# Two graph layers with neighbour lists: 114 list rounds in place of 119

## The chip, the cores and the metric

The kernel runs on one core of a Trainium2 chip. The metric is the device time of one execution in microseconds (us). The engines are TensorE (PE; its weight loads appear as PEld), VectorE (DVE), ScalarE (ACT), GpSimd (POOL) and SyncE (SP), which issues most of the DMAs.

## The reference

There are 3,327 nodes with 512 features each, and one adjacency matrix `adj` of 3,327 x 3,327. It is sparse and very uneven: the chance of an entry falls with the product of the roots of row and column number, so the first nodes have many neighbours and the last ones few. Cut to what matters:

```
h = relu(layernorm(x))
x = x + adj @ (relu(adj @ (h @ W1) + b1) @ W2) + b2            # layer 0
h = relu(layernorm(x))                                          # layer 1
ts     = adj @ h
attn_k = sigmoid([ts, h] @ W_k.T + b_k)                         # k = a, b: one number a node
s      = s_left[i] + s_right[j]                                 # from h @ W_sa and a_sa
e      = where(adj != 0, exp(-leaky_relu(s)), 0)
x_a    = (e / sum(e)) @ (h @ W_sa)
x_b    = adj @ (h @ W_gcnb) + b_gcnb
x = x + sigmoid(attn_a * x_a + attn_b * x_b)
```

Layer 1 needs, for every node, two weighted sums over its neighbours' rows of `h`: one with `adj`, one with `e`.

## The kernel before

The nodes are padded to 3,328 and cut into 26 blocks of 128. `adj` comes in transposed, and its columns (the nodes that receive) are cut into seven chunks: six of 512 and one of 256.

**First pass** (L494 to L536). For every chunk `c` the loop over the 26 blocks `j` loads a tile of `adj` (L510), multiplies it into `acc_u` (L511), and finds for each group of 32 columns the largest entry of each row (`most`, L515). From `most` the generator `make_lists` (L384) builds, one chunk later and a step at a time (`next(lists)`, L520), the list of the rows that have any entry in a group of 32 columns. These lists are what the change is about.

- A list has a fixed room: `rooms[i]` (L42) is the number of **rounds** of block `i`, and each round holds 64 entries (HALF) of each of the block's four groups of 32 columns. The four groups lie as two halves of the partitions (h) and two columns (q). Block 0, the hub, has no lists (0 rounds) and is computed densely. Places that a list doesn't fill get a row number beyond the matrix.
- In `make_lists` lists are built in batches of up to 18 rounds (`CW // NT`, L432), a batch being several (block, q) pairs. For each pair VectorE makes two threshold tiles `at` (L447), TensorE multiplies them into `p_list` (L459, two matmuls for each round and q), and for each batch VectorE runs five operations: `past` (L465), its sum `jb` (L470), and L471, L475 and L478, which leave row numbers in `row_h` and `row_a`. Between these steps the generator yields.
- `size` compares every list's length with its room (L414), and `overflow` is their maximum (L685).

GpSimd gathers by these row numbers (`gather`, L138; every gather in the profile has line L139). `gather_adj` (L148) yields, for blocks 1 to 25 in this order, one gather for each round and q: 128 pieces of 32 numbers of `adj` into the block's buffer `ae[i]`; pieces beyond the matrix are skipped, and the buffer was cleared before (L381). `gather_behind` (L173) issues one such gather at a time, tied behind a matmul of the dense passes: after two of three matmuls in the first pass (L521), after four of five in the second (L670).

**Second pass** (L658 to L699). The same tiles of `adj` are loaded again and multiplied into `acc_g` (L665). When a chunk is done, `make_h1` (L572) finishes layer 0 for its blocks, makes layer 1's `h`, and writes each block's rows, with one score as 513th column, to `h_rows` in DRAM (L588). In between, `add_hubs` (L619) sums up the hub block.

**Last stage** (L747 to L967). Blocks are taken from 25 down to 1. For each block:

- `attend` (L756) goes by segments of up to four rounds (`segments`, L121). For each round two gathers fetch 128 rows of 520 numbers each from `h_rows` (L774), places that are not filled fetching the last row (L475). Each round goes to one of 16 pairs of row buffers, which are used in turn (`pairs`, L753), so a gather waits until the sums of 16 rounds before have read its buffer. A block's first gather is also tied to the sums of three or four blocks before (`LEAD`, L777 to L779). Then VectorE and ScalarE compute `e` for the segment (L780, L784, L206 to L208, L789).
- `sums` (L796) adds up both sums in two PSUM banks: for each round four matmuls of 64x64 by 512 (L811), one for each quadrant of the array. In float32 each is two instructions in the profile, so a round is eight.
- `copy_out` (L880), `turn` (L816, transposes `ptt`, L823), `weigh` (L854: products `p_b`, L863, and `p_a`, L870) and `finish` (L719) make the output of a block. The loop at L918 writes the order out by hand: the products of the block before last stand ahead of the transposes of the last and of this block's sums. Block 1 (L941 to L967) has its segments' sums split: the first ahead of block 2's products, the others after.

If `overflow` is set, a branch at L970 computes layer 1 once more, densely, for all blocks. For the inputs given here the lists, counted with the reference's inputs, all fit into their rooms, before and after the change.

Of the kernel before, what the change touches and what calls it, by code (L numbers as in the profile page):

```python
# [37 lines left out]
def list_rooms(n_blocks):  # L38

    rooms = [0, 10, 8, 7, 6, 6] + 5 * [5] + 12 * [4]  # L42
    return (rooms + n_blocks * [3])[:n_blocks]


# [1 line left out]
def kernel(  # L47
# [23 lines left out]
    NCH = len(chunks)  # L71
    NG = NP // GW
    rooms = list_rooms(NB)
    first = [2 * sum(rooms[:i]) for i in range(NB)]
    NL = 2 * sum(rooms)
# [1021 lines left out]
```

## Time and profile before

| | |
|---|---|
| three runs | 788.9, 789.4 and 790.33 us, median 789.4 us |
| span of the profiled execution | 861.4 us |
| mean granted TensorE clock | 0.973 of full speed |
| TensorE busy | 796.8 us (92%) |
| VectorE, ScalarE, GpSimd busy | 519.0 (60%), 187.8 (22%), 514.0 us (60%) |
| DMA | 202.82 MB, 235 GB/s on average |
| first pass; second pass; last stage | until about 234; until about 448; until 861 us |
| gathers of `adj` (`ae`, L139) | 238, from 76.4 to 446.0 us |
| gathers of `h` rows (`hr` and `rows`, L139) | 150 and 88, from 459.9 to 817.5 us |
| sums at L809 | 952 instructions, 137.8 us busy in all |

The table is read from the page's first three parts and from the timeline. In the groups of instructions each row gives line, engine, operation, output and inputs with partitions x elements, count, busy time in us, mean ns of one, and the idle time ahead with what ended it. L809 is the matmul statement that begins there. Matmuls overlap, so the sum of the single durations is more than the busy time. A profiled execution is longer than a plain one.

### The profile page before, as it was taken

How to read it: one execution, taken by the hardware profiler on the slowest of the kernel's cores; microseconds unless marked ns; L12 is line 12 of the kernel's file. 1: busy time of each engine (PE TensorE's matmuls, PEld its weight loads, DVE VectorE, ACT ScalarE, POOL GpSimd, SP SyncE). 2: the span in 40 equal slices, each digit the busy share in tenths (PEclk: the TensorE clock that was granted, in tenths of full speed). 3: DMA queues.
4: the chain of work that ended last, by engine and by line, in shares of the span. 5: the costliest groups of instructions: out<-in, count | busy, mean ns of one | idle time of the engine just before them, and what ended most of it. 6: DMA issues, size and time to landing. Idle time of an engine off the chain costs nothing.

```text
span 861.4 us, 12424 instructions
## 1 busy us (share of the span) xinstructions
PE 796.8 (92%) x3707; PEld 426.9 (50%) x3707; DVE 519.0 (60%) x1668; ACT 187.8 (22%) x396; POOL 514.0 (60%) x533
## 2 busy tenths in 40 slices
PE   9999899999798999999989599699999999999795
PEld 8774444444443444444454366356555555445454
DVE  6777899998645776586565455254453534345342
ACT  6770000000002233033042022112221212112112
POOL 2302666666677777677755666676666767667600
PEclk9999999999799999999999799899999999999899
DMA  7787998887588998999957667777777777767620
GB/s 240 242 272 220 314 316 245 279 281 233 159 278 261 337 326 287 313 329 301 324 163 239 174 202 208 243 202 222 222 212 230 202 220 207 226 194 206 186 71 29
DMA packets 108220, 202.82 MB, mean 235 GB/s; under 512 B 17490, under 2 KB 31345, under 8 KB 108145
## 3 DMA queue, kind: packets, MB, share of 16 engines
q1 hardware_dynamic: 72800, 124.40, 44.0%
q0 software_dynamic: 26656, 66.41, 27.9%
q10 hardware_dynamic: 8688, 11.15, 3.9%
q8 instruction: 31, 0.51, 0.2%
q14 instruction: 45, 0.36, 0.1%
HBM read 182.22 MB, written 20.55 MB: 235 GB/s over the span
## 4 chain that ended last, share of the span: by engine, by line
PE 76%; DVE 8%; issue 6%; DMA 6%; ACT 1%; another core or an unknown queue 1%; SPq 0%; POOL 0%; DVEq 0%; POOLq 0%; ACTq 0%
PE acc L809 15%; PE acc_u L511 13%; PE p_b L863 12%; PE p_a L870 11%; PE acc_g L665 10%; DMA a<-in_adjT_dram 4%; PE acc_hub L624 3%; PE ptt L823 3%; DVE most L515 3%; PE pu L293 3%; PE p_list L459 2%; PE px L580 2%; DMA xb<-in_x_dram 1%; PE pt L285 1%; PE awake L100 1%
## 5 line engine op out<-in xcount | busy, mean ns | idle before, releaser
L139 POOL DMA_INDIRECT ae<-in_adjT_dram,row_a x238 | 256.2, 1076 | 161.6 <-issue 62.4
L139 POOL DMA_INDIRECT hr<-h_rows,row_h x150 | 154.6, 1031 | 70.5 <-issue 35.7
L511 PE MATMUL acc_u<-a,rows 128*128 128x512 f32 (+1 forms) x364 | 166.5, 588 | 3.2 <-DMA a<-in_adjT_dram 3.2
L665 PE MATMUL acc_g<-a,g 128*128 128x512 f32 (+1 forms) x364 | 157.9, 572 | 6.8 <-DMA a<-in_adjT_dram 6.6
L863 PE MATMUL p_b<-W_g_sb,tyT 128*128 128x257 f32 x416 | 105.6, 398 | 21.2 <-issue 20.2
L139 POOL DMA_INDIRECT rows<-h_rows,row_h x88 | 90.8, 1032 | 55.7 <-issue 18.9
L515 DVE TENSOR_REDUCE most<-a 128x16 f32<-128x512 f32 (+1 forms) x182 | 111.1, 639 | 7.7 <-DMA a<-in_adjT_dram 4.5
L665 PEld LDWEIGHTS acc_g<-a,g 128*128 128x128 f32 x364 | 67.7, 192 | 85.3 <-issue 62.6
L863 PEld LDWEIGHTS p_b<-W_g_sb,tyT 128*128 128x128 f32 x416 | 78.3, 194 | 57.6 <-issue 29.9
L870 PE MATMUL p_a<-W_sa_sb,tyT 128*128 128x512 f32 (+2 forms) x216 | 94.8, 582 | 1.0 <-issue 1.0
L511 PEld LDWEIGHTS acc_u<-a,rows 128*128 128x128 f32 x364 | 65.4, 196 | 50.5 <-issue 42.7
L809 PE MATMUL acc<-hr,ae 64*64 64x512 f32 x600 | 84.4, 608 | 2.6 <-issue 2.2
L838 DVE COPY tyT<-ptt 128x512 f32<-128x512 f32 x51 | 34.8, 685 | 68.4 <-PE ptt L823 27.6
L870 PEld LDWEIGHTS p_a<-W_sa_sb,tyT 128*128 128x128 f32 x216 | 41.4, 192 | 40.4 <-issue 38.5
L809 PE MATMUL acc<-rows,ae 64*64 64x512 f32 x352 | 53.4, 596 | 2.9 <-issue 2.8
L809 PEld LDWEIGHTS acc<-hr,ae 64*64 64x64 f32 x600 | 34.8, 136 | 36.5 <-issue 33.8
L208 DVE SCALAR_TENSOR_TENSOR ae<-ae 128x256 f32<-128x256 f32 (+2 forms) x36 | 12.8, 377 | 61.8 <-ACT ae L207 39.2
L728 ACT ACTIVATE f<-f 128x2 f32<-128x2 f32 x26 | 5.3, 203 | 192.1 <-DVE vb L734 71.6
L302 ACT ACTIVATE gT<-acc_u,b_col 128x512 f32<-128x512 f32 (+1 forms) x7 | 4.6, 657 | 163.9 <-issue 78.7
L735 DVE TENSOR_TENSOR vb<-p_b,bg_row 128x257 f32<-128x257 f32 x26 | 11.1, 426 | 42.9 <-PE acc L809 28.6
L559 DVE SCALAR_TENSOR_TENSOR junk<-rows,w_rows 128x512 bf16<-128x512 f32 x52 | 35.6, 685 | 1.7 <-ACT rows L201 0.3
L583 DVE TENSOR_TENSOR xb<-px,xb 128x512 f32<-128x512 f32 x26 | 17.0, 684 | 31.3 <-PE px L580 22.7
(142 smaller groups left out, 936.4 us busy)
## 6 DMA issues: line engine op xcount, KB each, us to landing
a<-in_adjT_dram SPq DMA_DIRECT2D x325, 256.0 KB
h_rows<-rows SPq DMA_DIRECT2D x26, 260.0 KB
x<-in_x_dram SPq DMA_DIRECT2D x26, 256.0 KB
xb<-in_x_dram SPq DMA_DIRECT2D x26, 256.0 KB
x<-xb ACTq DMA_DIRECT2D x26, 256.0 KB
x1b<-x SPq DMA_DIRECT2D x26, 256.0 KB
out_dram<-va SPq DMA_DIRECT2D x25, 256.0 KB
ae<-in_adjT_dram,row_a POOLq DMA_INDIRECT x238
```

Source lines behind the costliest of these rows:

```text
L139: return nc.gpsimd.indirect_dma_start(out=dst, out_offset=None, in_=table, in_offset=bass.IndirectOffsetOnAxis(ap=rows, axis=0), bounds_ch ...
L293: nc.tensor.matmul(pu[:, :HID], hT[:, k, :], W1_sb[:, k, :], start=(k == 0), stop=(k == KD - 1))
L511: added = nc.tensor.matmul(acc[:, :w], u[j], a[:, :w], start=(j == 0), stop=(j == NB - 1))
L515: nc.vector.tensor_reduce(most[:, : w // GW, j], a[:, :w].rearrange("p (b i) -> p b i", i=GW), axis=AX.X, op=ALU.max, apply_absolute_value ...
L559: return nc.vector.scalar_tensor_tensor(junk, h, 1.0, w_rows[:, s, :], op0=ALU.mult, op1=ALU.mult, accum_out=into)
L624: nc.tensor.matmul(acc_hub[k], s, hrow[i % NR][:, :D], start=(i == 0), stop=(i == NB - 1))
L665: added = nc.tensor.matmul(acc[:, :w], g[j], a[:, j % per, :], start=(j == 0), stop=(j == NB - 1))
L809: added = nc.tensor.matmul(taken[i]["acc"][h][q * HALF : (q + 1) * HALF, :], both[half_p, q * n + k, :], taken[i][k0][k][half_p, q, :D], s ...
L823: moved = nc.tensor.transpose(pt[:, k * P : (k + 1) * P], ty[h][:, k * P : (k + 1) * P], ident)
L838: last = nc.vector.tensor_copy(dst, src)
L863: nc.tensor.matmul(p_b[n][:, :WH], tyT[:, k, 0, :], W_g_sb[:, k, n * WH : (n + 1) * WH], start=(k == 0), stop=(k == KD - 1),)
L870: last = nc.tensor.matmul(p_a[:, c0:c1], tyT[:, k, 1, :], W_sa_sb[:, k, c0:c1], start=(k == 0), stop=(k == KD - 1),)
```

## The change

One line of `list_rooms` is changed:

```diff
-    rooms = [0, 10, 8, 7, 6, 6] + 5 * [5] + 12 * [4]
+    rooms = [0, 9, 8, 7, 6, 6] + 5 * [5] + 8 * [4]
     return (rooms + n_blocks * [3])[:n_blocks]
```

Block 1 has nine rounds in place of ten, blocks 19 to 22 have three in place of four, and all other blocks what they had: 119 rounds become 114. The rooms set, besides the sizes of several buffers,

- the number of gathers: two of `adj` and two of `h` rows for each round, so 228 and 228 in place of 238 and 238;
- the number of matmuls: four list matmuls and four sums (eight instructions) for each round;
- the segments: block 1's are three, three and three rounds in place of four, three and three; blocks 19 to 22 keep one each;
- the batches in which lists are built: chunk 0 (blocks 1 to 3) has batches of 18, 16 and 14 rounds in place of 10, 18, 15 and 7; chunk 4 has 16 and 14 in place of 16 and 16; chunk 5 has 18 and 6 in place of 16 and 14;
- which of the 16 row buffers a block's rounds get, since fewer are taken before it.

SyncE's instructions are the same in number, kind and order, and so are ScalarE's, but for five smaller shapes.

## The prediction

> **What bounds the kernel now.** I read the profile in this order: the page's chain that ended last, the groups of instructions, the chain in order of time for the last stage, GpSimd's timeline there, and busy time by windows.
>
> ```profile
> PE 76%; DVE 8%; issue 6%; DMA 6%; ACT 1%; another core or an unknown queue 1%; SPq 0%; POOL 0%; DVEq 0%; POOLq 0%; ACTq 0%
> ...
> L809 PE MATMUL acc<-hr,ae 64*64 64x512 f32 x600 | 84.4, 608 | 2.6 <-issue 2.2
> ...
> L809 PE MATMUL acc<-rows,ae 64*64 64x512 f32 x352 | 53.4, 596 | 2.9 <-issue 2.8
> ```
>
> TensorE carries three quarters of the path. The 119 rounds are its 952 matmul instructions of L809: eight each, 137.8 us together, 1.16 us a round on average. The chain in order of time shows what one round is worth (start, length, what):
>
> ```profile
> 507.50 2.63 PE acc L809 x22
> 510.13 3.67 PE p_b L863 x16
> 513.80 3.43 PE p_a L870 x8
> 518.32 3.49 PE acc L809 x30
> 521.81 1.28 PE p_b L863 x5
> 523.28 2.63 PE p_b L863 x11
> 525.92 3.43 PE p_a L870 x8
> 530.43 3.49 PE acc L809 x30
> ```
>
> Block 23 (three rounds) starts its sums at 507.50 and block 22 (four) at 518.32; the next start is 530.43. TensorE goes from sums to products to sums with hardly a gap, so this stage is bound by TensorE. Three rounds take 2.63 us, four 3.49: 0.87 us a round. The end of the kernel reads the same way, with block 1's first segment of four rounds at 827.95 and its other six at 838.75:
>
> ```profile
> 827.95 3.49 PE acc L809 x30
> 831.44 3.67 PE p_b L863 x16
> 835.10 3.43 PE p_a L870 x8
> 838.75 5.31 PE acc L809 x46
> ```
>
> GpSimd, which issues the gathers, is not the bound of the four-round blocks:
>
> ```profile
> 519.58 1.00 POOL L139 DMA_INDIRECT hr<-h_rows,row_h  x1 [0.30 <-issue]
> 520.88 0.99 POOL L139 DMA_INDIRECT hr<-h_rows,row_h  x1 [0.30 <-issue]
> 523.83 0.99 POOL L139 DMA_INDIRECT hr<-h_rows,row_h  x1 [1.96 <-remote]
> 525.13 1.00 POOL L139 DMA_INDIRECT hr<-h_rows,row_h  x1 [0.31 <-issue]
> ```
>
> A gather goes out every 1.30 us, eight in 10.4 us, and then GpSimd waits 1.4 to 2.7 us once in each block, for sums that free a row buffer or that its pace is tied to. The last view is one window of 5 us (busy time of PE, PEld, DVE, ACT and POOL, clock, DMA share, GB/s):
>
> ```profile
> 480.00:485.00 5.00, 0.00 (x0) 0.00 (x0) 0.00 (x0) 0.00 (x0) 3.00 (x3) 0.50 0.72 200
> ```
>
> Here TensorE, VectorE and ScalarE all stand still while gathers go on. Two more such stops lie near 549 to 559 and 797 to 808.
>
> **What the Trainium skill says.** "TensorEngine Tiling (Array Packing)", Tiling Modes: the array can work as four independent 64x64 tiles. The trace agrees: 32 instructions of some 589 ns each take 3.49 us, 109 ns apart. "DMA: Bandwidth & Descriptors", SWDGE vs HWDGE vs iDMA: descriptors of DMAs issued from GpSimd are made by software on that engine; the trace's 1.0 us for every gather, empty or full, agrees. "Runtime: NRT & Kernel Launch", Instruction fetch mechanics: each engine's instructions are fetched by DMA in blocks of 16 KiB. The page of before has an instruction queue with 31 packets for 0.51 MB, 16.5 KB each. I take this as a possible cause of the stops; no run shows it.
>
> **The change, part by part.**
>
> Lengths, counted from the inputs: block 1's longest list has 529 entries, room falls from 640 to 576; the longest in blocks 19 to 22 has 183, room falls from 256 to 192. So no list overflows, the branch at L970 is not taken, and all ten removed gather pairs were padding: the adjacency rows lie out of bounds, the feature rows all point at row 3327.
>
> 1. Blocks 19 to 22, one round less each. Starts of sums of three-round blocks lie 10.91 and 10.82 us apart (496.59, 507.50, 518.32). Those of eight four-round blocks away from the stops lie 12.11, 11.93, 11.97, 11.99, 12.24, 11.86, 11.94 and 12.33 apart, 12.05 on average. The difference is 1.18 us: 0.87 of sums, and 0.31 of gaps inside the products (as at 521.81 to 523.28) that three-round blocks do not show. I take 1.18; bounds 0.87 (the gaps stay) and 1.18. Four blocks: 4.7 us.
> 2. Block 1, nine rounds. Its segments go from 4, 3, 3 to 3, 3, 3, so the first sums lose a round, 0.87 us; VectorE is done with them before 829, and with the later segments by 834.7, 4 us before they are used. The upper bound is 1.18. 0.9 us.
> 3. The gathers. Ten feature gathers of 128 rows of 2,080 bytes go, 13 us of GpSimd's cadence and 2.7 MB. Hidden: GpSimd waits for TensorE in each of these blocks. Ten adjacency gathers go from the two dense passes, where each is paced behind a matmul (L525, L671); the last now goes out at 446.0, at the end of the pass, and will go out about 12 matmul steps earlier. The next work on that queue is the first feature gather at 459.9, which waits for the last h_rows, so this gains nothing.
> 4. The lists. In chunk 0 four batches (10, 18, 15, 7 rounds) become three (18, 16, 14). By the rows of L465, L470, L471, L475 and L478 for these shapes VectorE's work falls from 5.9 to 5.0 us; chunks 4 and 5 save 0.1 and 0.3 (16 and 14 become 16 and 14; 18 and 6). The threshold operations L447 stay (380 ns at 640, 296 at 256, 304 at 192). TensorE loses 20 list matmuls, 0.5 us at about 25 ns apart. Together 1.8 us in the first pass, where VectorE is 93% busy (97.5 of 105 us from 102 to 207) and the chain changes between it, TensorE and loads. The first lists are now made a step later, but the first gather's slot in the loop (j = 4) is the same. Bounds: 0 and 1.8; I take 0.5.
> 5. VectorE and ScalarE also lose about 0.7 and 0.06 us per shortened block. Hidden: VectorE is busy 6.4 of 12.1 us in that window. Clearing smaller buffers on GpSimd lies before its first gather at 76.4, for which it waited 47 us: nothing.
>
> The sum is 4.7 + 0.9 + 0.5 = 6.1 us from the profiled span of 861.4 us. The three plain runs are 72 us shorter (789.4), and what makes up that difference is not known from here; the saved work is array time at full clock, so I take the same 6.1 us from 789.4: **783.3 us**. With all bounds low it is 4.4 us (785.0), with all high 4 x 1.18 + 1.18 + 1.8 = 7.7 us (781.7).
>
> **Rivals.**
>
> - *The gathers bind without the profiler.* For: between waits they go out without a pause, and the DMA engines are 71 to 79% busy here. Against: GpSimd waits in every block, and blocks of three rounds, 7.8 us of gathers, take 10.9. Then 10 x 1.30 = 13 us go: 776.4.
> - *The head start is lost again.* In blocks 10 to 6 (five rounds) ten gathers take 13.0 us and a wait of some 1.8 follows, in a period of about 14.6, with TensorE at half pace in the first sums. If TensorE arrives there earlier and only waits longer for rows, points 2 and 4 stay: 1.4 us, 788.0. Against: GpSimd has eight gathers less to make before, 10.4 us.
> - *One stop more (the slower side).* Each stop costs about 10.4 us on TensorE (476.4 to 486.8). If they depend on where instruction refills meet dense gathers, about 100 fewer TensorE instructions shift where they fall. One more anywhere after 460 gives 789.4 - 6.1 + 10.4 = 793.7. It decides once added stop time exceeds 6.1 us. For: three in 390 us; against: nothing shows that their number follows the instruction count, or that they occur without the profiler.
> - *One stop fewer*: 789.4 - 6.1 - 10.4 = 772.9.
> - *The branch is taken after all*: 7 x 26 x 8 dense matmuls at 0.86 us, 1,250 us more. The counted lists exclude it.
>
> **How the numbers follow.** Chances: the sum 0.66; gathers bind 0.08; head start lost 0.09; a stop more 0.10; a stop fewer 0.07. I leave out the last two, 0.17: the range is 776.4 to 788.0, and the likeliest case's own is 781.7 to 785.0. A change of over 0.2%, 1.6 us, is about what a measurement of this kernel can tell from none. Faster: 0.66 + 0.08 + 0.07 = 0.81; within 0.2%: 0.09; slower: 0.10.
>
> **What would show it.** Right: sums of blocks 22 to 19 with 24 instructions in about 2.63 us and starts about 10.9 us apart; block 1's first sums 2.6 us; chunk 0's lists in three batches; 912 instructions at L809. Wrong: starts still 12 us apart in those blocks (a wait took the place), longer gaps ahead of sums at five-round blocks (head start lost), a fourth stop of all three engines, or a drop near 13 us. Point 4 is wrong if the first pass ends later than 234 us.

## The result, and the profile after

The changed kernel takes 781.3 us (median of four runs, 779.5 to 783.3) against 789.9 us; the ratio is 0.988, 95% interval 0.983 to 0.993. A second measurement gave 0.988 again (0.985 to 0.991), 9.7 us. The forecast was 783.3 us, 6.1 us faster.

The profiled execution of after has a span of 780.7 us and lies within the plain runs, so a profiled execution isn't longer as such. That of before, 861.4 us, was an unusually slow one: a second profile of the same kernel (before_again, below) has 797.6 us, and the three stops are not in it. So before is read from before_again from here on. First the chain that ended last and the groups of sums, of after:

```profile
span 780.7 us, 12235 instructions
...
PE 82%; DMA 7%; DVE 7%; issue 1%; ACT 1%; POOL 0%; SPq 0%; POOLq 0%; ACTq 0%; DVEq 0%
...
L809 PE MATMUL acc<-hr,ae 64*64 64x512 f32 x560 | 68.0, 607 | 0.0
...
L809 PE MATMUL acc<-rows,ae 64*64 64x512 f32 x352 | 42.5, 594 | 2.5 <-issue 1.8
```

There are 912 instructions at L809, 110.5 us busy, 0.97 us a round in place of the 1.16 of the first profile. The same lines of before_again give 116.3 us for 119 rounds, 0.98 us: most of the fall from 137.8 us is the disturbance, not the change. The chain in order of time of after (start, length, what), at blocks 23 and 22:

```profile
478.06 2.63 PE acc L809 x22
480.69 3.67 PE p_b L863 x16
484.35 3.43 PE p_a L870 x8
488.87 2.63 PE acc L809 x22
491.50 3.67 PE p_b L863 x16
495.17 3.43 PE p_a L870 x8
```

Block 22 now has 22 pieces in 2.63 us, and starts are 10.81 us apart. In before_again four-round blocks start 11.67 us apart, without the gap inside the products, as here at block 22:

```profile
498.09 3.49 PE acc L809 x30
501.58 3.67 PE p_b L863 x16
505.25 3.43 PE p_a L870 x8
509.76 3.49 PE acc L809 x30
```

The difference is 0.86 us, TensorE's work alone.

GpSimd's timeline shows what the first profile hid. This is before_again, at blocks of four rounds and near the end:

```profile
540.06 1.00 POOL L139 DMA_INDIRECT rows<-h_rows,row_h  x1 [0.30 <-issue]
541.37 1.00 POOL L139 DMA_INDIRECT rows<-h_rows,row_h  x1 [0.30 <-issue]
542.68 1.00 POOL L139 DMA_INDIRECT hr<-h_rows,row_h  x1 [0.30 <-issue]
543.98 1.00 POOL L139 DMA_INDIRECT hr<-h_rows,row_h  x1 [0.30 <-issue]
...
717.35 1.00 POOL L139 DMA_INDIRECT hr<-h_rows,row_h  x1 [0.30 <-DMA hr<-h_rows,row_h]
718.65 1.00 POOL L139 DMA_INDIRECT hr<-h_rows,row_h  x1 [0.30 <-PE acc L809]
```

From 451.14 to 765.74 no gather after the first starts more than 0.31 us after the one before has ended; most go out 1.30 us apart, the farthest 1.82. GpSimd never waits for sums: **it is behind**, and the 238 gathers take 314.6 us. After has pauses again, in its three-round blocks:

```profile
498.37 0.99 POOL L139 DMA_INDIRECT hr<-h_rows,row_h  x1 [0.30 <-issue]
502.68 0.99 POOL L139 DMA_INDIRECT hr<-h_rows,row_h  x1 [3.31 <-PE acc L809]
```

Here a gather waits 3.31 us for sums of an earlier block: the stream has caught up. After 502.68 no gather waits any more. Now the end of the stage in the chain in order of time. Before_again, blocks 4 to 2:

```profile
714.16 4.43 PE acc L809 x38
718.59 0.06 issue
718.65 5.01 DMA hr<-h_rows,row_h
...
730.47 1.25 issue
731.72 3.77 DMA hr<-h_rows,row_h
...
736.99 4.06 DMA hr<-h_rows,row_h
...
744.59 1.76 issue
746.35 9.67 PE acc L809 x64
```

And after_again (a second profile of after):

```profile
706.45 5.21 PE acc L809 x46
711.66 3.67 PE p_b L863 x16
...
719.84 6.06 PE acc L809 x54
725.90 3.67 PE p_b L863 x16
...
734.11 1.27 issue
735.38 7.10 PE acc L809 x64
```

A "DMA hr" piece is a gather's flight, from its issue at 718.65 to its landing at 723.66, on which a block's scores wait. In before_again the chain leaves TensorE at block 4 and runs through gathers until block 2's sums. It puts the gather of 718.65 down to sums that ended at 718.59, but that gather goes out 1.30 us after the last, as any other: the sums didn't hold it up. In after_again the chain stays on TensorE, but for 1.27 us ahead of block 2's sums. There, too, their scores have just waited for a gather:

```profile
733.33 0.23 DVE L780 TENSOR_TENSOR ae<-s_left,hr 128x64 f32<-128x64 f32 x1 [2.33 <-DMA hr<-h_rows,row_h]
```

How much of this TensorE itself stands still is in busy time by windows, of before_again and then of after_again, over blocks 4 to 2 (columns as in the prediction):

```profile
715.00:747.00 32.00, 27.71 (x174) 16.29 (x170) 14.21 (x54) 6.26 (x14) 24.69 (x25) 0.96 0.81 219
```

```profile
706.00:736.00 30.00, 28.70 (x191) 17.19 (x193) 15.37 (x56) 6.26 (x14) 22.99 (x24) 1.00 0.81 223
```

TensorE idles 4.3 us of the first and 1.3 us of the second. But the wait costs more than that. Block 2's sums, 64 instructions, take 9.67 us in before_again and 7.10 in after_again. This is the start of them in before_again:

```profile
746.35:751.00 4.65, 4.65 (x24) 1.68 (x28) 3.81 (x13) 0.20 (x1) 3.72 (x4) 0.50 0.94 296
```

TensorE is busy throughout, but at a granted clock of 0.50 (the third number from the end). In gathers_only (below), where TensorE doesn't stop ahead of these sums, the clock there is 1.00 and they take 6.92 us. So in this execution the late gathers cost 4.3 us of standing still and about 2.75 us of slow sums, 7 us in all. After's first profile lies between: 1.77 us of waiting ahead of block 2, then 8.79 us of sums.

From the first gather of h rows to the end, before_again takes 346.5 us, after 338.8 and after_again 339.8.

### The profile page after: what moved, and what is told of

Read it like the earlier page. It is cut to its first block, busy times and chain, and to the rows that moved or that the text cites. A ratio compares the mean times of both kernels' runs of the same rounds, so it can differ in the third digit from the quotient of the medians.

```text
span 780.7 us, 12235 instructions
## 1 busy us (share of the span) xinstructions
PE 755.4 (97%) x3647; PEld 415.5 (53%) x3647; DVE 517.5 (66%) x1658; ACT 185.5 (24%) x396; POOL 489.8 (63%) x513
## 4 chain that ended last, share of the span: by engine, by line
PE 82%; DMA 7%; DVE 7%; issue 1%; ACT 1%; POOL 0%; SPq 0%; POOLq 0%; ACTq 0%; DVEq 0%
PE acc_u L511 16%; PE acc_g L665 14%; PE acc L809 13%; PE p_b L863 12%; PE p_a L870 11%; DMA a<-in_adjT_dram 6%; PE ptt L823 3%; PE pu L293 3%; PE acc_hub L624 2%; PE px L580 2%; PE p_list L459 2%; PE pt L285 1%; DVE junk L559 1%; DVE xb L583 1%; PE awake L100 1%
## 5 line engine op out<-in xcount | busy, mean ns | idle before, releaser
L139 POOL DMA_INDIRECT ae<-in_adjT_dram,row_a x228 | 244.2, 1071 | 145.2 <-DVE most L515 49.1
L139 POOL DMA_INDIRECT hr<-h_rows,row_h x140 | 143.5, 1025 | 47.0 <-issue 27.4
L511 PE MATMUL acc_u<-a,rows 128*128 128x512 f32 (+1 forms) x364 | 164.0, 580 | 1.5 <-DMA a<-in_adjT_dram 1.5
L863 PE MATMUL p_b<-W_g_sb,tyT 128*128 128x257 f32 x416 | 97.1, 386 | 0.8 <-ACT tyT L836 0.5
L863 PEld LDWEIGHTS p_b<-W_g_sb,tyT 128*128 128x128 f32 x416 | 76.6, 189 | 30.8 <-DVE ae L206 7.3
L809 PE MATMUL acc<-hr,ae 64*64 64x512 f32 x560 | 68.0, 607 | 0.0
L809 PE MATMUL acc<-rows,ae 64*64 64x512 f32 x352 | 42.5, 594 | 2.5 <-issue 1.8
L809 PEld LDWEIGHTS acc<-hr,ae 64*64 64x64 f32 x560 | 29.8, 136 | 23.4 <-issue 22.9
L302 ACT ACTIVATE gT<-acc_u,b_col 128x512 f32<-128x512 f32 (+1 forms) x7 | 4.6, 656 | 154.8 <-PE acc_u L511 97.9
L696 DVE TENSOR_TENSOR xb<-xb,b_row 128x512 f32<-128x512 f32 x26 | 17.7, 690 | 29.7 <-DMA xb<-in_x_dram 24.1
L823 PEld LDWEIGHTS ptt<-ident,ty 128*128 128x128 f32 x208 | 24.2, 141 | 14.2 <-issue 12.9
```

Source lines behind the costliest of these rows:

```text
L139: return nc.gpsimd.indirect_dma_start(out=dst, out_offset=None, in_=table, in_offset=bass.IndirectOffsetOnAxis(ap=rows, axis=0), bounds_ch ...
L511: added = nc.tensor.matmul(acc[:, :w], u[j], a[:, :w], start=(j == 0), stop=(j == NB - 1))
L809: added = nc.tensor.matmul(taken[i]["acc"][h][q * HALF : (q + 1) * HALF, :], both[half_p, q * n + k, :], taken[i][k0][k][half_p, q, :D], s ...
L823: moved = nc.tensor.transpose(pt[:, k * P : (k + 1) * P], ty[h][:, k * P : (k + 1) * P], ident)
L863: nc.tensor.matmul(p_b[n][:, :WH], tyT[:, k, 0, :], W_g_sb[:, k, n * WH : (n + 1) * WH], start=(k == 0), stop=(k == KD - 1),)
```

## The experiments

Each ratio is to the kernel before; times in us are the ratio applied to its median in the same measurement (793.8 to 794.1 us). Single profiles of one kernel differ by several us in where the last stage begins, so totals are taken from the timed runs and the profiles are read within a stage.

### before_again and after_again: the two kernels once more

> The kernel before, unchanged: a second profile and the spread of the measurement. If the three stops of TensorE, VectorE and ScalarE in the profile of before belong to that one execution, this profile has a span near 788 us, four-round blocks 11.7 us apart in place of 12.05, and a ratio of 1.000 within 0.2%. If they belong to the kernel, the span is again near 860 us.

Measured: 1.000 (0.998 to 1.002), span 797.6 us. The stops belong to the one execution; the four-round period is 11.67 us, as expected for that case.

> The changed kernel again, for a narrower interval. Sum of the parts (work of five rounds on TensorE 4.3 us, lists 0.5 to 1.8 us): 4.8 to 6.1 us below before, ratio 0.992 to 0.994. If gathers bind (13 us) 0.983; if the 8.5 us measured first are real, 0.989.

Measured: 0.988 (0.985 to 0.991), 9.7 us. The interval, 7.1 to 12.3 us, leaves out both the sum of the parts and ten gathers' 13 us.

### late_only and early_only: the two halves of the change

late_only keeps lists of 119 rounds and issues the ten empty gathers of adj into a spare buffer; `used` holds the shorter rooms:

```diff
-        n = -(-rooms[i] // SEG)
-        cuts = [-(-rooms[i] * k // n) for k in range(n + 1)]
+        n = -(-used[i] // SEG)
+        cuts = [-(-used[i] * k // n) for k in range(n + 1)]
...
+            for k in range(used[i], r):
...
+                    yield gather(spare, adj_groups, row_a[:, f : f + 1], NP * NG - 1)
```

> Only the last stage is shortened: lists are built with 119 rounds, all 238 gathers of adj are issued (the ten empty ones into a spare buffer), and the last stage runs 114 rounds. If the gain is TensorE's work there: 4.3 us below before (0.9945). If the lists carry half or more of the gain: 2 us or less. If gathers of h rows bind: 8 us or more.

Measured: 0.992 (0.989 to 0.995), 6.4 us (4.1 to 8.7). The interval takes in TensorE's 4.3 us and the gathers' 8, so this run doesn't tell the two apart.

early_only has the rooms the other way round, with constant row numbers where the list has no round:

```diff
-                            row_a[:, f : f + 1], NP * NG - 1,
+                            row_a[:, f : f + 1] if k < r else beyond, NP * NG - 1,
...
-                            hr[k][:, q, :], h_dram[:, :], row_h[:, f : f + 1], NP - 1
+                            hr[k][:, q, :], h_dram[:, :],
+                            row_h[:, f : f + 1] if k0 + k < r else last_row_id, NP - 1,
```

> The opposite half: lists are built with 114 rounds, and the last stage still runs 119, the five empty ones with a constant row number; all 238 gathers of adj are issued. If the lists matter as forecast: 0.5 us below before, at most 1.8 us (0.998 to 0.9995). If they carry what the forecast missed: about 4 us (0.995).

Measured: 0.996 (0.994 to 0.998), 3.4 us (1.9 to 5.0). The halves add up to 9.8 us, the gain of the whole within the intervals. The lists are worth more than the 0.5 us forecast, and the interval begins just above its upper bound of 1.8.

### gathers_only and sums_only: which resource the last stage pays for

gathers_only leaves out the ten empty gathers of h rows and nothing else; the five empty rounds are still summed:

```diff
-                hr.append(next(pairs))
-                for q in range(2):
+                full = k0 + k < used[i]
+                hr.append(next(pairs) if full else hr[-1])
+                for q in range(2 if full else 0):
```

> Lists, gathers of adj and all 119 rounds of sums as before; only the ten empty gathers of h rows are left out (the five empty rounds read the row buffer of the round before, weighted with zeros). If TensorE alone bound the last stage, as the prediction had it: no gain (1.000). If gathers bound it alone: 8 us or more (0.990 or less). New theory, that gathers bind its end only, where TensorE waits for rows at blocks 3 and 2: TensorE's waits of some 3.5 us go and its work stays, 0.9955 (3 to 4 us).

Measured: 0.993 (0.992 to 0.995), 5.2 us (3.7 to 6.7), with not one TensorE instruction less. The 3 to 4 us expected left out the slow sums after the wait; the 7 us of before_again's one profile lie just above the interval. The path through gathers at the end is gone; blocks 3 and 2 now read:

```profile
724.90 6.06 PE acc L813 x54
730.97 3.67 PE p_b L867 x16
734.63 3.43 PE p_a L874 x8
739.15 6.92 PE acc L813 x62
```

sums_only is late_only with the ten empty gathers put back, into row buffers that nothing reads:

```diff
+            for k in range(used[i], r if k1 == used[i] else 0):
+                unread = next(pairs)
+                for q in range(2):
...
+                        gathered[0] = gather(
+                            unread[:, q, :], h_dram[:, :], row_h[:, f : f + 1], NP - 1
+                        )
```

> The opposite: the last stage has 114 rounds of sums, and all 119 rounds of gathers of h rows still go out, the ten empty ones into buffers in their turn that nobody reads; lists and gathers of adj as before. If TensorE bound the stage: 4.3 us below before (0.9945). New theory: gathers set when blocks 3 to 1 can be summed, so TensorE only waits longer for them; 0.9 us for block 1's round and at most 2.6 us for its last two gathers, which nothing waits for any more (0.997 to 0.999).

Measured: 1.003 (1.001 to 1.005): 2.3 us **slower** than before (1.0 to 3.7), with 40 sums fewer. TensorE's 4.3 us are worth nothing while the gathers stay. Its chain in order of time keeps the pieces of before:

```profile
715.88 4.80 DMA hr<-h_rows,row_h
...
730.73 3.83 DMA hr<-h_rows,row_h
734.63 4.05 DMA hr<-h_rows,row_h
```

So the theory that TensorE bounds the last stage falls, and the new one holds in kind. Its number missed: sums_only should have been a little faster than before, and is a little slower. Its profile doesn't show why (its last stage takes 345.0 us); that stays open.

The other profiles agree. From the first gather of h rows to the end, the five with 238 such gathers take 345.0 to 346.5 us: before_again, adj_only, early_only, early_tight, and sums_only with its 114 rounds of sums. The four with 228 take 337.3 to 339.8: after, after_again, late_only, and gathers_only with all 119 rounds (339.2). The stage goes by its gathers far more than by its sums.

### block1_only and four_blocks_only: which rounds

The edits are the change's own, one list of rooms each:

```diff
+    rooms = [0, 9, 8, 7, 6, 6] + 5 * [5] + 12 * [4]      # block1_only
+    rooms = [0, 10, 8, 7, 6, 6] + 5 * [5] + 8 * [4]      # four_blocks_only
```

> Only block 1's part of the change: nine rounds in place of ten, with one list batch less in chunk 0. By TensorE's work and the list's cost: 0.9 + 0.9 us (0.998). If gathers bind the stage's end: two gathers less before block 1 can be summed, 2.6 us, and up to 0.9 us of lists, 0.9955 to 0.997; TensorE's waits at blocks 3 and 2 stay, since the gathers ahead of these are the same.

Measured: 0.995 (0.993 to 0.997), 4.0 us (2.5 to 5.6). The stream of 236 gathers takes 312.0 us in place of 314.6, 2.6 us less as expected, and flights stay on the path ahead of block 2, also as expected.

> Only blocks 19 to 22's part: three rounds in place of four. By TensorE's work: 3.4 us and up to 0.5 of lists (0.995). If gathers bind the stage's end: eight gathers, 10.4 us, less ahead of blocks 3 and 2, so TensorE's waits there go from some 14 us to under 4; but TensorE, which saves 3.4 us, is then the bound, so 6 to 7 us in all (0.991 to 0.993).

Measured: 0.992 (0.990 to 0.995), 6.2 us (4.0 to 8.3), at the low edge of 6 to 7. In its chain blocks 4 to 2 run on TensorE but for 1.48 us ahead of block 2's sums (the 14 us of waits in the expectation are far more than the 4.3 us that TensorE stood still in before_again), and one flight remains, for block 1's last gather:

```profile
747.45 0.05 PE acc L809
...
751.62 4.77 DMA hr<-h_rows,row_h
```

Both edits together end this as well. The two add up to 10.2 us, after's 9.7 within the intervals.

### adj_only: the empty gathers of adj

```diff
-                    for k in range(k0, k1):
+                    for k in range(k0, min(k1, used[i])):
```

> Only the ten empty gathers of adj are left out, lists and last stage as before. Prediction's step 3: nothing (1.000 within 0.2%), since they are paced behind matmuls and end long before the first gather of h rows. If the shorter second pass in the profiles of after (206.5 and 208.9 us against 210 to 213) came from them: 2 to 4 us (0.995 to 0.9975).

Measured: 1.000 (0.999 to 1.002). They cost nothing that these runs can tell, as step 3 had it, and the shorter second pass seen in two profiles earns nothing through them.

### early_tight: more of the lists

early_only with list rooms of 108 rounds, `[0, 9, 7, 6] + 5 * [5] + 10 * [4]`; gathers and last stage as before.

> As early_only (lists shortened, 238 gathers of adj and 119 rounds in the last stage), with lists of 108 rounds: two batches fewer than before in place of one, 44 list matmuls fewer in place of 20. By the cost of the rows (VectorE about 0.9 us a batch, TensorE 25 ns a matmul): some 3 us below before (0.996). If early_only's 3.4 us are the lists' slope: some 7 us (0.991). If 3.4 us were mostly chance: nearer 2 us (0.9975).

Measured: 0.994 (0.990 to 0.997), 5.0 us (2.3 to 7.8). All three readings lie inside the interval or at its edge; it shows again that shorter lists gain, and not how much a batch or a round is worth.

### tight108: the change taken further

Lists, gathers and last stage with the same 108 rounds.

> The same edit as the change, taken as far as these lists allow with rooms that never grow from a block to the next: 108 rounds, blocks 2 and 3 with seven and six, 4 to 8 with five, 9 to 18 with four. If each round is worth 1.7 us as in the change: 10 us below after, 0.975 of before. If only TensorE's 0.87 us a round is left once the gathers no longer bind: 5.2 us below after, 0.981. If the cadence of gathers binds the end again: 2.6 us a round, 0.968.

Measured: 0.977 (0.975 to 0.980), 776.5 us, 17.9 us below before and some 8 us below after, the best version measured. Six more rounds bring 1.4 us each, between TensorE's 0.87 and the gathers' 2.6: both have become shorter, and so have the lists, and the run doesn't tell their shares apart. Its chain shows no gather's flight in blocks 4 to 1. Its rooms leave little to spare for other inputs: blocks 4 and 5 have 310 and 318 entries for 320 places.

## Why the prediction was right, and where it was not

The direction, the range and nearly the time held; the main mechanism did not. That 783.3 us came within 2 us of the first measurement is in part luck: the medians lie 8.6 us apart there, and the second gave 9.7 us, against a forecast of 6.1 whose own bounds ended at 7.7. The signs that were to show it right (10.81 us between starts, sums of 2.63 us, 912 instructions) all came, but they follow from the edit and would have come under the rival too.

- **Steps 1 and 2 (TensorE's rounds, 4.7 and 0.9 us).** The 0.87 us a round was right, and the 0.31 us of gaps belonged to that first profile: 11.67 against 10.81 us. But in before the price isn't paid in TensorE's time: sums_only saves that time and gains nothing. Only once the gathers are fewer can shorter sums count, and then for little: late_only gives 6.4 us and gathers_only 5.2, with intervals that overlap, and last stages of 337.3 and 339.2 us.
- **Step 3, feature gathers ("Hidden: GpSimd waits for TensorE in each of these blocks").** This is the step that failed. The waits were read from an execution in which TensorE was held up; in before_again GpSimd does not wait. gathers_only gains 5.2 us where the step had zero. The rival "the gathers bind", given a chance of 0.08, named the mechanism, and its 13 us were too much. The shorter stream catches up with TensorE in the three-round blocks and pauses there, so from first gather to last it loses 8.6 us (after: 306.0 us, from 441.9 to 747.9, in place of 314.6) or 5.6 us (after_again: 309.0), and TensorE's own work then sets all of the end but for the short wait ahead of block 2.
- **Step 3, gathers of adj.** Right: adj_only 1.000.
- **Step 4 (lists, 0.5 us, at most 1.8).** Mis-sized: early_only gives 3.4 us (1.9 to 5.0). Its last stage is as long as before's (345.8 us against 346.5), so the gain lies in the passes ahead of it. Where in them is open. The chunk in which chunk 0's lists are built, from one `gT` (L302) to the next, takes 26.56 or 26.57 us in six profiles with ten rounds for block 1 (before_again among them) and 26.02 to 26.48 in five with nine, but 26.68 in block1_only, which has nine as well; the other chunks differ by more between profiles with the same lists.
- **Step 5.** Not tested alone; nothing in the runs needs it.
- **The 72 us between profile and plain runs.** The prediction carried a sum from the one to the other as if both had the same bound. They had not: in the slow execution TensorE was held up, and that hid that GpSimd was late.
- **The stops.** No stop more or fewer decided anything: they do not recur in the later profiles. Before_again has the same instruction queue (31 packets, 0.51 MB), so the number of fetches alone doesn't bring them about; their cause stays open. Only the first held TensorE for the 10.4 us given to each: from 549 to 559 and from 797 to 808 it was busy 5.1 and 6.5 us.

The error in the bound and the small price of the lists both made the sum too low, 6.1 for 9.7 us, and the gaps that don't exist made up 1.2 us of it. In the experiments' terms the 9.7 us are gathers of h rows, 5.2, and lists, 3.4; the 1.1 us left over are within the intervals.

## What to carry to other kernels

When the profiled span is 9% above the plain runs, take a second profile before reading from it which engine waits for which: a producer that waits has time to spare only if its consumer ran at its usual pace. Where a producer (here the gathers) and a consumer (the sums) share buffers that are used in turn, both look busy; leaving out the transfers while keeping the arithmetic, and the opposite, tells in two runs which one is paid for. When TensorE waits, look also at its clock after the wait. Padding is worth cutting first where its transfers go through the queue that is behind.

## What the runs showed of the hardware

A gather of 128 rows whose indices all name the same row takes the same place in the stream as any other: in early_only those of the constant row at 499.97 and 501.27 take 1.00 us each on GpSimd, and the next go out 1.30 and 1.31 us later. Whether GpSimd or the DMA engines, 81 to 83% busy at 219 to 245 GB/s from 700 to 747 us of before_again, set that cadence was not tried. Gathers of adj whose indices are all out of bounds cost nothing measurable where they are paced behind other work (adj_only, 1.000).

Before block 2's sums, TensorE stood still for 2.5 us and, after 1.4 us of work, for 1.8 us in before_again, and the next 4.65 us ran at a granted clock of 0.50. After one wait of 1.77 us in after they took 8.79 us, and after one of 1.27 us in after_again 7.10, close to the 6.92 without a wait. What sets the clock in between, no run here shows.
